# Attention with a residual on one core: the second scores of a step moved behind the values, and the last pair's final products in halves

## The chip, the cores and the metric

The kernel runs on one core of a Trainium2 chip. The core has five engines with a queue of their own each: TensorE (PE, matmuls), VectorE (DVE), ScalarE (ACT), GpSimd (POOL) and SyncE (SP, which here starts transfers). Work on one engine runs in the order in which it was put there; engines wait for each other through semaphores. The metric is the device time of one execution in microseconds (us), the median of the runs shown.

## The reference

`x` has 64 batches of 128 tokens with 512 features. For each batch the kernel adds to `x` the result of an attention layer with 16 heads of 64 features that share one key and one value, and with one extra "null" key and value (`cond`) ahead of the 128 real ones:

```python
xn = layernorm(x, g_in)
q = (xn @ Wq).reshape(b, n, H, DH).transpose(0, 2, 1, 3) * scale
kv = xn @ Wkv
k, v = (kv[..., :DH], kv[..., DH:])
...
sim = jnp.einsum('bhid,bjd->bhij', q, k)
...
sim = jnp.where(causal_mask, neg, sim)
...
attn = jax.nn.softmax(sim, axis=-1)
out = jnp.einsum('bhij,bjd->bhid', attn, v)
out = out.transpose(0, 2, 1, 3).reshape(b, n, INNER)
out = out @ Wo
return layernorm(out, g_out)
```

All of it is in float32. The output is `x` plus this.

## The kernel before, in words

The order of all work is written out by hand: nothing is rescheduled, and each engine's queue holds its instructions in the order in which the functions below are called. Semaphore waits are derived from the tiles that instructions read and write.

Batches go through in pairs. Step `d` (1 to 32) has three pairs in flight: the scores and the softmax of batches `a = 2d` and `b = 2d + 1`, the values and the output projection of the pair `p = 2d - 2`, and the normalisation, residual and store of the pair `l = 2d - 4`. Up to step 29 a step is `turn(d)` and `body(d)`, with the query products of a later pair between. Steps 30 and 31 have no query products left: they are `turn_end(d)` and `body_end(d)`, where `last` is true for step 31. Step 32 is `turn_end(32)`, which only makes the values of the last pair, and `body_last()`. The change touches these last three steps.

What a step does, by the names that follow:

- `scores(b, hf)` is the product of queries and keys for a half `hf` of the query rows: the first half (`hf` 0) needs 64 keys, the second (`hf` 1) 128. They go to PSUM rooms: those of the first halves are `ps_y` "Y" and `ps_w` "w" for a, `ps_q` "a" and `ps_w` "w" for b; the second half of a has the bank `ps_s` "s", that of b `ps_y` "X" and `ps_q` "c". `scores_add` (DVE, L667 and L669) adds mask and bias, `scores_max` (DVE, L674) takes the row maximum, `exps` (ACT, L683) the exponentials, eight rows of heads to a half, `rinv` (DVE, L701) the reciprocal of the sums, and `scale` (POOL, L705) multiplies by it.
- `blocks_T` (DVE, L721) transposes 32 by 32 blocks of the scaled weights for the product with the values; `lo` and `hi` are its two halves of rows.
- `values_rooms` gives the pair p four PSUM rooms, "a", "w", "Y", "w", each one tile for both batches. `values` (PE, L781) makes attention weights times values. `values_out_one` copies the result into the tile `oT` and adds the null value: rooms 0 and 2 by ACT (L800), rooms 1 and 3 by DVE (L798).
- The output projection of a pair is a Strassen-like scheme of seven products of 128 x 512 by 512 x 256: `out_product(p, k)` (PE, L868) is product k, four matmuls of 256 columns (two records each in the trace). `out_sum(p, k)` (L848) makes the sums of `oT` that they need: sum 0 by DVE in these steps, sums 1 to 3 by POOL; product 6 needs sum 1, product 7 sum 2, product 4 sum 3. Products 1, 6, 7 and 4 accumulate in one PSUM bank, and between them the bank is copied (`out_keep`: ACT L882, DVE L880) or added (`out_part`: DVE L898, ACT L896). Products 5 and 3 share another bank.
- `late_stats`, `late_nmr` and `late_norm` (DVE, ACT) normalise an output, `late_gain` (DVE, L1093) multiplies by `g_out`, `late_residual` (POOL, L1096) adds `x` and starts the store. `load_res` (SP) fetches that `x`.

In `turn_end(31)` as it is before, the second half of the scores of batch b stands ahead of the values, and the pending `blocks_T` of the pair p (`late_T`) stands between the row maxima. `body_end(30)` ends with the gains and residual adds of its pair l, batches 56 and 57. `body_last` ends with products 7 and 4 of the last pair, each over all 256 columns, the statistics (`bn_stats`) of each half of the output as it is ready, `late_first` and `late_second` for batch 62, and then the same two passes, and the stores, for batch 63 in halves.

Of the kernel before, what the change touches and what calls it, by code (L numbers as in the profile page):

```python
# [8 lines left out]
FP = mybir.dt.float32  # L9
U8 = mybir.dt.uint8  # L10
AF = mybir.ActivationFunctionType
ALU = mybir.AluOpType
# [5 lines left out]
def kernel(  # L18
# [698 lines left out]
    def blocks_T(b, lo=0, hi=R8):  # L717

        if lo == 0:
            sbs[b] = hp.tile([P, 6, R8, Q], FP, tag="sb", name=f"sb_{b}")  # L720
        nc.vector.transpose(  # L721
            sbs[b][:, :, lo:hi].rearrange("p j e q -> p e j q"),
            S[b][:, lo:hi, 1 : ROW - 1].rearrange("p e (j k) -> p e j k", k=Q),
        )
# [122 lines left out]
        )[k]  # L847
        eng.tensor_tensor(o, a, b, op)  # L848

    def out_product(p, k, pool, tag, start=True):  # L850
        key = "y" + tag
        if start and pool is ps_s:
            two = ps_s.tile([P, 2, DIM], FP, tag="s", name=f"py_{p}_{k}_s")
            prod[key] = two[:, 0, 0:HE]
        elif start:
            prod[key] = pool.tile([P, HE], FP, tag=tag, name=f"py{tag}_{p}_{k}")
        a, b = oT[p], oT[p + 1]
        h, w = {
            1: (a[:, 0], e11),
            2: (a[:, 1], e21),  # L860
            3: (a[:, 1], e22),
            4: (b[:, 1], sums_e[3]),
            5: (yS.get(p), sums_e[0]),
            6: (a[:, 0], sums_e[1]),
            7: (b[:, 0], sums_e[2]),
        }[k]
        for c in range(HC):
            nc.tensor.matmul(  # L868
                prod[key],
                h[:, c, :],  # L870
                w[:, c, :],
                start=(start and c == 0),
                stop=(c == HC - 1),
                skip_group_check=not start,
            )
# [8 lines left out]
    def out_part(b, e, tag, name=None):  # L884
        if b not in ys:
            if B - 6 <= b < B - 2:
                ys[b] = gp.tile(
                    [P, DIM], FP, tag=f"xS{b - B + 7}", name=f"y_{b}", bufs=1
                )
            elif b == B - 1:  # L890
                ys[b] = gp.tile([P, DIM], FP, tag="xT", name=f"y_{b}")
            else:
                ys[b] = hp.tile([P, DIM], FP, tag="y", name=f"y_{b}", bufs=3)
        o = ys[b][:, lo_e if e == 0 else hi_e]
        if name is None:
            nc.scalar.copy(o, prod["y" + tag])  # L896
        else:
            nc.vector.tensor_tensor(o, prod["y" + tag], kept.pop(name), ALU.add)  # L898
# [52 lines left out]
        )  # L951

    PAIRS = B // 2
    late_T = []

    def turn(d):

# [26 lines left out]
    def turn_end(d):  # L984

        a, b, p = 2 * d, 2 * d + 1, 2 * d - 2
        if d == PAIRS:
            blocks_T(*late_T.pop())
            late_nmr(p - 3)
            late_norm(p - 3)  # L990
            late_gain(p - 4)
            late_residual(p - 4, nc.gpsimd)
            values_rooms_apart(p)
            result_room(p)
            for m in (p, p + 1):
                values(m)
                values_out_one(m)
            return
        scores(a, 0, ((ps_y, "Y"), (ps_w, "w")))
        scores(b, 0, ((ps_q, "a"), (ps_w, "w")))  # L1000
        scores(a, 1)
        scores(b, 1, ((ps_y, "X"), (ps_q, "c")))
        scores_add(a, 0)
        scores_add(b, 0)
        scores_max(a, 0)
        if late_T:
            blocks_T(*late_T.pop())
        scores_max(b, 0)
        scores_add(a, 1)
        po = values_rooms(p)  # L1010
        values(p)
        values(p + 1)
        if d + 1 < PAIRS:
            bias_add(a + 2)
        exps(a, 0, 0, 7)
        result_room(p)
        values_out_one(p, (0, 1))
        exps(a, 0, 7)
        values_out_one(p + 1)
        values_out_one(p, (2, 3))  # L1020
        rinv(a, 0)
        out_sum(p, 0, nc.vector)
        scores_add(b, 1)

    def body_first():

# [72 lines left out]
    def body_end(d):  # L1099

        a, b, p, l = 2 * d, 2 * d + 1, 2 * d - 2, 2 * d - 4
        last = d + 1 == PAIRS
        lo, hi = (0, R8 // 2), (R8 // 2, R8)
        for r in range(p, B if last else p + 2):
            load_res(r)
        scores_max(a, 1)
        late_stats(l if last else l + 1)
        out_product(p, 1, ps_s, "s")
        exps(b, 0, 0, 4)
        out_keep("s", "yp1", "yp1")  # L1110
        exps(b, 0, 4)
        out_sum(p, 1)
        scale(a, 0)
        out_product(p, 2, ps_w, "w")
        out_part(p, 0, "w", "yp1")
        out_sum(p, 2)
        pair_pow(l if last else l + 1)
        rinv(b, 0)
        out_sum(p, 3)
        scale(b, 0)  # L1120
        scores_max(b, 1)
        out_product(p, 6, ps_s, "s", start=False)
        out_keep("s", "yu2", "yu2")
        exps(a, 1, *lo)
        rinv(a, 1, *lo)
        scale(a, 1, *lo)
        late_nmr(l)
        out_product(p, 5, ps_y, "Y")
        exps(a, 1, *hi)
        rinv(a, 1, *hi)  # L1130
        scale(a, 1, *hi)
        out_keep("Y", "yp5", "yp5")
        if last:
            late_stats(l + 1)
        else:
            late_nmr(l + 1)
        out_product(p, 7, ps_s, "s", start=False)
        exps(b, 1, *lo)
        out_part(p + 1, 1, "s", "yp5")
        rinv(b, 1, *lo)  # L1140
        scale(b, 1, *lo)
        blocks_T(a, *lo)
        blocks_T(a, *hi)
        out_product(p, 3, ps_y, "Y", start=False)
        exps(b, 1, *hi)
        rinv(b, 1, *hi)
        scale(b, 1, *hi)
        out_part(p, 1, "Y", "yu2")
        late_norm(l)
        if last:  # L1150
            pair_pow(l + 1)
        else:
            late_norm(l + 1)
        blocks_T(b, *lo)
        late_T.append((b, *hi))
        out_product(p, 4, ps_s, "s", start=False)
        out_part(p + 1, 0, "s")
        if not last:
            for m in (l, l + 1):
                late_gain(m)  # L1160
                late_residual(m, nc.gpsimd)

    def body_last():

        p = B - 2
        y = p - 2
        st = [
            small.tile([P, 2, 6], FP, tag=f"stl{i}", name=f"stl{i}", bufs=1)
            for i in range(2)
        ]  # L1170
        out_sum(p, 0, nc.vector)
        late_stats(y)
        out_product(p, 1, ps_q, "c")
        out_keep("c", "yp1", "yp1")
        out_sum(p, 1)
        pair_pow(y)
        late_stats(y + 1)
        out_product(p, 2, ps_w, "w")
        out_part(p, 0, "w", "yp1")
        nc.vector.bn_stats(st[0][:, 0], ys[p][:, lo_e])  # L1180
        out_sum(p, 3)
        pair_pow(y + 1)
        out_product(p, 5, ps_y, "Y")
        out_keep("Y", "yp5", "yp5")
        late_first(y)
        out_sum(p, 2)
        out_product(p, 6, ps_q, "c", start=False)
        late_gain(y - 1)
        late_nmr(y + 1)
        late_norm(y + 1)  # L1190
        late_second(y)
        out_keep("c", "yu2", "yu2")
        late_residual(y - 1, nc.gpsimd)
        out_product(p, 3, ps_y, "Y", start=False)
        late_gain(y + 1, nc.gpsimd)
        late_residual(y + 1, nc.gpsimd)
        out_part(p, 1, "Y", "yu2")
        nc.vector.bn_stats(st[0][:, 1], ys[p][:, hi_e])
        out_product(p, 7, ps_q, "c", start=False)
        out_part(p + 1, 1, "c", "yp5")  # L1200
        mv, rstd = last_stats(p, st[0])
        nc.vector.bn_stats(st[1][:, 1], ys[p + 1][:, hi_e])
        out_product(p, 4, ps_q, "c", start=False)
        yn[p] = mv, rstd
        late_first(p)
        late_second(p)
        x0 = prod["yc"]
        y = ys[p + 1]
        nc.vector.bn_stats(st[1][:, 0], x0)
        mv, rstd = last_stats(p + 1, st[1])  # L1210
        for half, src in ((hi_e, y[:, hi_e]), (lo_e, x0)):
            nc.vector.scalar_tensor_tensor(
                y[:, half], src, mv[:, 0:1], gob[:, half], ALU.subtract, ALU.mult
            )
        r = res.pop(p + 1)
        for half, queue in ((hi_e, nc.sync), (lo_e, nc.scalar)):
            nc.vector.scalar_tensor_tensor(
                y[:, half], y[:, half], rstd, r[:, half], ALU.mult, ALU.add
            )
            queue.dma_start(out=out[p + 1][:, half], in_=y[:, half])  # L1220
# [400 lines left out]
```

## Time and profile before

| | |
|---|---|
| median of 3 runs | 1029.53 us (1029.39 to 1029.55) |
| the profiled execution | 1029.77 us |
| its span in the trace | 1027.9 us |
| PE, PEld (weight load) busy | 1018.8 us (99%), 899.6 us (88%) |
| DVE, ACT, POOL busy | 799.0, 699.1, 745.2 us |
| `turn_end(31)` | scores from about 987.1, product 1 of the pair at 993.64 |
| `body_last` | product 1 at 1008.98, last product at 1020.19 |
| DVE's last pass | 1023.92 to 1024.80 |

Times of the trace count from the start of the span. A row of a timeline has the start, the length, the engine, the line of the kernel before, the operation, the tiles out and in, their shapes, how many instructions were merged into the row, and, in brackets, the idle time of that engine before it with what ended it. The chain of work that ended last is the path followed back from the last instruction; its rows have the start, the length on the path, engine, tile and line. `PE` is the matmul pipeline, `PEld` the weight load beside it.

### The profile page before, as it was taken

How to read it: one execution, taken by the hardware profiler on the slowest of the kernel's cores; microseconds unless marked ns; L12 is line 12 of the kernel's file. 1: busy time of each engine (PE TensorE's matmuls, PEld its weight loads, DVE VectorE, ACT ScalarE, POOL GpSimd, SP SyncE). 2: the span in 40 equal slices, each digit the busy share in tenths (PEclk: the TensorE clock that was granted, in tenths of full speed). 3: DMA queues.
4: the chain of work that ended last, by engine and by line, in shares of the span. 5: the costliest groups of instructions: out<-in, count | busy, mean ns of one | idle time of the engine just before them, and what ended most of it. 6: DMA issues, size and time to landing. Idle time of an engine off the chain costs nothing.

```text
span 1027.9 us, 31287 instructions
## 1 busy us (share of the span) xinstructions
PE 1018.8 (99%) x12345; PEld 899.6 (88%) x12345; DVE 799.0 (78%) x1774; ACT 699.1 (68%) x2805; POOL 745.2 (72%) x579
## 2 busy tenths in 40 slices
PE   9999999999999999999999999999999999999997
PEld 9888888888888888888888888888888888888886
DVE  6877777877778877788777788777888777877697
ACT  5766678666678666786666786666776667856582
POOL 4997768686686857758677686776868678586676
PEclk9999999999999999999999999999999999999999
DMA  6514152141522315233141421415223151230211
GB/s 212 144 56 127 66 152 87 53 129 64 163 77 92 99 59 167 68 108 114 45 150 67 134 99 49 140 63 158 83 76 108 60 172 69 94 90 25 82 63 63
DMA packets 73834, 100.85 MB, mean 98 GB/s; under 512 B 32212, under 2 KB 36056, under 8 KB 71896
## 3 DMA queue, kind: packets, MB, share of 16 engines
q1 hardware_dynamic: 73392, 98.47, 30.8%
q8 instruction: 96, 1.57, 0.6%
q14 instruction: 50, 0.41, 0.1%
q10 hardware_dynamic: 296, 0.40, 0.1%
HBM read 63.19 MB, written 33.55 MB: 94 GB/s over the span
## 4 chain that ended last, share of the span: by engine, by line
PE 97%; DVE 1%; POOL 1%; issue 0%; POOLq 0%; DVEq 0%
PE pa L515 20%; PE pyX L868 19%; PE pyY L868 10%; PE pc L515 10%; PE po L781 7%; PE pkv L363 6%; PE pyw L868 5%; PE pl L581 4%; PE pq L450 3%; PE ps L652 3%; PE sc_X L652 2%; PE sc_Y L652 2%; PE py_s L868 1%; PE sc_a L652 1%; PE sc_w L652 1%; PE busy L1453 1%
## 5 line engine op out<-in xcount | busy, mean ns | idle before, releaser
L683 ACT ACTIVATE s<-s,nmax 128x65 f32<-128x65 f32 (+1 forms) x1024 | 372.0, 367 | 62.4 <-DVE nmax L674 62.4
L705 POOL TENSOR_TENSOR s<-s,rinv 128x512 f32<-128x512 f32 (+1 forms) x132 | 190.8, 1448 | 151.0 <-DVE rinv L701 151.0
L617 POOL TENSOR_TENSOR s<-biasp,mneg 128x1552 f32<-128x1552 f32 (+1 forms) x65 | 205.9, 3171 | 51.2 <-DVE s L667 38.2
L683 ACT ACTIVATION_READ_ACCUMULATOR s<-s,nmax 128x1 f32 x1024 | 194.6, 190 | 0.0
L533 ACT COPY qT<-pa 128x256 f32<-128x256 f32 x59 | 22.0, 373 | 147.2 <-PE pa L515 147.2
L674 DVE TENSOR_REDUCE nmax<-s 128x8 f32<-128x1032 f32 (+1 forms) x128 | 121.4, 949 | 0.1
L515 PE MATMUL pa<-xS,wq 128*128 128x256 f32 x472 | 121.2, 379 | 0.0
L721 DVE STREAM_TRANSPOSE sb<-s 128x1536 f32<-128x1536 f32 (+1 forms) x68 | 113.5, 1672 | 2.0 <-POOL s L705 2.0
L868 PE MATMUL pyX<-wT,oT 128*128 128x256 f32 x464 | 109.7, 379 | 0.0
L868 PE MATMUL pyX<-wo,oT 128*128 128x256 f32 x464 | 109.7, 379 | 0.0
L515 PEld LDWEIGHTS pa<-xS,wq 128*128 128x128 f32 x472 | 87.2, 190 | 11.1 <-issue 0.2
L868 PEld LDWEIGHTS pyX<-wo,oT 128*128 128x128 f32 x464 | 86.0, 190 | 10.5
L868 PEld LDWEIGHTS pyX<-wT,oT 128*128 128x128 f32 x464 | 85.9, 190 | 10.6
L848 POOL TENSOR_TENSOR oT<-oT 128x512 f32<-128x512 f32 x64 | 80.6, 1277 | 3.9 <-PE pyw L868 1.6
L781 PE MATMUL po<-sb,vr 32*64 32x256 f32 (+1 forms) x4064 | 81.4, 300 | 0.0
L781 PEld LDWEIGHTS po<-sb,vr 32*64 32x64 f32 x4064 | 70.9, 130 | 8.4 <-issue 5.3
L597 DVE TENSOR_TENSOR qT<-pl,kp 128x128 f32<-128x128 f32 x112 | 31.2, 279 | 58.6 <-PE pl L581 56.0
L800 ACT ACTIVATE oT<-po,nv 128x512 f32<-128x512 f32 (+1 forms) x127 | 73.7, 654 | 0.1
L536 DVE TENSOR_TENSOR qT<-pc,ku 128x256 f32<-128x256 f32 x118 | 48.5, 411 | 32.5 <-PE pc L515 18.1
L281 POOL TENSOR_TENSOR rstd<-rstd,nhalf 128x1 f32<-128x1 f32 x64 | 35.1, 555 | 52.5 <-DVE rstd L280 43.6
L363 PE MATMUL pkv<-xT,wkv 128*128 128x256 f32 x256 | 63.3, 391 | 0.0
L527 ACT COPY ku<-pa 128x256 f32<-128x256 f32 x118 | 43.4, 368 | 28.3 <-PE pa L515 23.8
(186 smaller groups left out, 2419.2 us busy)
## 6 DMA issues: line engine op xcount, KB each, us to landing
res<-in_x_dram SPq DMA_DIRECT2D x64, 256.0 KB
x<-in_x_dram SPq DMA_DIRECT2D x63, 256.0 KB
out_dram<-y SPq DMA_DIRECT2D x63, 256.0 KB
xd<-xb SPq DMA_DIRECT2D x14, 1024.0 KB
xT<-xd SPq DMA_DIRECT2D x56, 256.0 KB
vr<-vd SPq DMA_DIRECT2D x64, 128.0 KB
kT<-kT SPq DMA_DIRECT2D x32, 64.0 KB
vd<-vb SPq DMA_DIRECT2D x32, 64.0 KB
```

Source lines behind the costliest of these rows:

```text
L363: nc.tensor.matmul(pkv, wkv[:, kc, :], xT[g][:, t : t + 2, kc, :], start=(kc == 0), stop=(kc == KC - 1),)
L515: nc.tensor.matmul(prod[tag], w[:, kc, f * P : (f + 1) * P], t[:, :, kc, :], start=(start and kc == 0), stop=(kc == HK - 1), skip_group_ch ...
L617: nc.gpsimd.tensor_tensor(S[b][:, :, keys], biasp[:, :, keys], mneg[:, t, keys] .unsqueeze(1) .broadcast_to([P, R8, keys.stop - keys.start ...
L652: nc.tensor.matmul(home[r][u * DH : (u + 1) * DH, f, :], qT[g, f, t // 2][rows, t % 2, hf, u], kT[rows, 0 : nk // Q, t, :], start=True, st ...
L674: nc.vector.tensor_reduce(nmax[b][:, hf], S[b][:, :, WITH_NULL[hf]], AX.X, ALU.max, negate=True)
L683: nc.scalar.activation(row, row, AF.Exp, bias=nmax[b][:, hf, k : k + 1], accum_out=rsum[b][:, hf, k : k + 1],)
L705: nc.gpsimd.tensor_tensor(sv, sv, rinvs[b, hf][:, lo:hi].unsqueeze(2).broadcast_to([P, hi - lo, sv.shape[2]]), ALU.mult,)
L721: nc.vector.transpose(sbs[b][:, :, lo:hi].rearrange("p j e q -> p e j q"), S[b][:, lo:hi, 1 : ROW - 1].rearrange("p e (j k) -> p e j k", k=Q),
L781: nc.tensor.matmul(po[s][rows, to : to + n], vr[g][quad, t, PLACE[j], :], sb[quad, slots, r * NF : (r + 1) * NF, :], start=(turn == 0), st ...
L800: nc.scalar.activation(to, src, AF.Identity, bias=nv2)
L848: eng.tensor_tensor(o, a, b, op)
L868: nc.tensor.matmul(prod[key], h[:, c, :], w[:, c, :], start=(start and c == 0), stop=(c == HC - 1), skip_group_check=not start,)
```

## The change

In `turn_end` (steps 30 and 31): `scores(b, 1)` goes behind the values; the transposes of b's upper rows, which step 31 did between its maxima, are done at the end of `body_end(30)`; `scores_max(b, 0)` goes behind the copies of the values; these copies (`values_out_one`) go in after the first and the fourth of the exponentials of `a`, batch by batch; DVE's `out_sum(p, 0)` goes ahead of `rinv(a, 0)`; and the gains and residual adds that `body_end(30)` did at its end are done at the end of `turn_end(31)`. In `body_last`: products 7 and 4 are each made as two halves of 128 columns, with the add, or the statistics, of a half behind it; the statistics of batch 62 are closed between the two halves of product 7.

```diff
-    def out_product(p, k, pool, tag, start=True):
+    def out_product(p, k, pool, tag, start=True, cols=slice(0, HE)):
...
             nc.tensor.matmul(
-                prod[key],
+                prod[key][:, cols],
                 h[:, c, :],
-                w[:, c, :],
+                w[:, c, cols],
...
     # out_part: the tile y of the last batch is made in body_last instead
-            elif b == B - 1:
-                ys[b] = gp.tile([P, DIM], FP, tag="xT", name=f"y_{b}")
...
     # turn_end
         scores(a, 1)
-        scores(b, 1, ((ps_y, "X"), (ps_q, "c")))
         scores_add(a, 0)
         scores_add(b, 0)
         scores_max(a, 0)
-        if late_T:
-            blocks_T(*late_T.pop())
-        scores_max(b, 0)
         scores_add(a, 1)
-        po = values_rooms(p)
+        values_rooms(p)
         values(p)
         values(p + 1)
+        scores(b, 1, ((ps_y, "X"), (ps_q, "c")))
         if d + 1 < PAIRS:
             bias_add(a + 2)
-        exps(a, 0, 0, 7)
+        exps(a, 0, 0, 1)
         result_room(p)
-        values_out_one(p, (0, 1))
-        exps(a, 0, 7)
+        values_out_one(p)
+        exps(a, 0, 1, 4)
         values_out_one(p + 1)
-        values_out_one(p, (2, 3))
+        scores_max(b, 0)
+        exps(a, 0, 4)
+        out_sum(p, 0, nc.vector)
         rinv(a, 0)
-        out_sum(p, 0, nc.vector)
         scores_add(b, 1)
+        for m in late_gains:
+            late_gain(m)
+            late_residual(m, nc.gpsimd)
+        late_gains.clear()
...
     # body_end
         blocks_T(b, *lo)
-        late_T.append((b, *hi))
+        if last:
+            late_T.append((b, *hi))
+        else:
+            blocks_T(b, *hi)
+            late_gains.extend((l, l + 1))
         out_product(p, 4, ps_s, "s", start=False)
         out_part(p + 1, 0, "s")
-        if not last:
-            for m in (l, l + 1):
-                late_gain(m)
-                late_residual(m, nc.gpsimd)
...
     # body_last
-        out_product(p, 7, ps_q, "c", start=False)
-        out_part(p + 1, 1, "c", "yp5")
-        mv, rstd = last_stats(p, st[0])
-        nc.vector.bn_stats(st[1][:, 1], ys[p + 1][:, hi_e])
-        out_product(p, 4, ps_q, "c", start=False)
-        yn[p] = mv, rstd
+        y = ys[p + 1] = gp.tile([P, DIM], FP, tag="xT", name=f"y_{p + 1}")
+        x0 = prod["yc"]
+        yp5 = kept.pop("yp5")
+        for i in range(2):
+            out_product(p, 7, ps_q, "c", start=False, cols=parts[i])
+            nc.vector.tensor_tensor(
+                y[:, parts[2 + i]], x0[:, parts[i]], yp5[:, parts[i]], ALU.add
+            )
+            if i == 0:
+                yn[p] = last_stats(p, st[0])
         late_first(p)
+        for i in range(2):
+            nc.vector.bn_stats(st[1][:, 2 + i], y[:, parts[2 + i]])
         late_second(p)
-        x0 = prod["yc"]
-        y = ys[p + 1]
-        nc.vector.bn_stats(st[1][:, 0], x0)
+        for i in range(2):
+            out_product(p, 4, ps_q, "c", start=False, cols=parts[i])
+            nc.vector.bn_stats(st[1][:, i], x0[:, parts[i]])
         mv, rstd = last_stats(p + 1, st[1])
```

The lines that name a function (`# turn_end` and the like) and `...` stand for what is left out.

More of the change, by code (lines that the diff above doesn't have):

```diff
@@ L953 @@
     PAIRS = B // 2
-    late_T = []
+    late_T, late_gains = [], []
     def turn(d):
@@ L1167, in body_last @@
         st = [
-            small.tile([P, 2, 6], FP, tag=f"stl{i}", name=f"stl{i}", bufs=1)
+            small.tile([P, 2 + 2 * i, 6], FP, tag=f"stl{i}", name=f"stl{i}", bufs=1)
             for i in range(2)
         ]
+        parts = [slice(i * P, (i + 1) * P) for i in range(4)]
         out_sum(p, 0, nc.vector)
```

## The prediction

> **What bounds the kernel now.** I read the page first: the shares of the engines, and the chain of work that ended last.
>
> ```profile
> PE 1018.8 (99%) x12345; PEld 899.6 (88%) x12345; DVE 799.0 (78%) x1774; ACT 699.1 (68%) x2805; POOL 745.2 (72%) x579
> PE 97%; DVE 1%; POOL 1%; issue 0%; POOLq 0%; DVEq 0%
> ```
>
> TensorE (PE) is busy for 99% of the span and makes 97% of the chain. So a change can only win what PE still idles, and anything that makes PE wait is paid in full. PE's timeline from step 30 on (start, length, what it is, and in brackets the idle time before it with what ended it):
>
> ```profile
> 974.79 1.97 PE L868 MATMUL py_s<-wo,oT 128*128 128x256 f32 x8 [0.61 <-DVE oT L798]
> ...
> 978.32 1.89 PE L868 MATMUL py_s<-wT,oT 128*128 128x256 f32 x8
> ...
> 993.64 1.97 PE L868 MATMUL py_s<-wo,oT 128*128 128x256 f32 x8 [0.78 <-DVE oT L798]
> 995.44 1.89 PE L868 MATMUL pyw<-wo,oT 128*128 128x256 f32 x8
> 997.17 1.89 PE L868 MATMUL py_s<-wT,oT 128*128 128x256 f32 x8
> ...
> 1008.98 1.99 PE L868 MATMUL pyc<-wo,oT 128*128 128x256 f32 x8
> ...
> 1017.71 1.89 PE L868 MATMUL pyc<-wo,oT 128*128 128x256 f32 x8
> 1020.19 1.99 PE L868 MATMUL pyc<-wT,oT 128*128 128x256 f32 x8 [0.58 <-DVE y L898]
> ```
>
> Three gaps are in reach: 0.61 and 0.78 us ahead of product 1 in steps 30 and 31, and 0.58 us ahead of product 4 in the last pair, 1.97 us in all. Whole products follow each other every 1.73 us (997.17 less 995.44).
>
> **Step 30: what the second scores behind the values do.** These rows are of the chain, VectorE (DVE) and ScalarE (ACT):
>
> ```profile
> 970.58 0.41 DVE L667 TENSOR_TENSOR s<-sc_a,s 128x256 f32<-128x256 f32 x1
> 970.85 0.10 PE sc_X L652 x2
> 971.72 2.41 PE po L781 x121
> 974.16 1.66 DVE L798 TENSOR_SCALAR oT<-po,nv 128x256 f32<-128x256 f32 x4 [0.83 <-PE po L781]
> ...
> 971.63 0.35 ACT L683 ACTIVATE s<-s,nmax 128x65 f32<-128x65 f32 x1 [2.34 <-DVE nmax L674]
> 971.97 0.34 ACT L683 ACTIVATE s<-s,nmax 128x65 f32<-128x65 f32 x1
> 974.16 0.47 ACT L800 ACTIVATE oT<-po,nv 128x256 f32<-128x256 f32 x1
> 975.93 0.36 ACT L683 ACTIVATE s<-s,nmax 128x65 f32<-128x65 f32 x1
> 977.26 0.36 ACT L882 COPY kyp<-py_s 128x256 f32<-128x256 f32 x1
> ```
>
> The values write the PSUM rooms that the first score sums read, so they can begin once the last of these adds ends, 970.58 + 0.41 = 970.99. Before, the second scores (970.85 to 971.72, 0.87 us) covered that. Now the values run from 971.05 to 973.46 and the scores to about 974.4; product 1 starts there, 0.4 us sooner than 974.79. So far the gap is filled.
>
> The price is on ACT. The row of DVE at 974.16 had idled 0.83 us for the values, and begins 0.03 us after the end of both batches' values (971.72 + 2.41 = 974.13), though it reads the first batch only. Each room is one tile for both batches, and a reader waits for its last matmul. The changed kernel puts ACT's copies of the first batch (`values_out_one(p)`) after one exponential instead of seven. ACT does one from 971.63, then stands until 973.5. Four copies and one exponential took 975.93 - 974.16 = 1.77 us; six more exponentials at 0.335 us (971.97 less 971.63, rounded) make 2.0. The first half's exponentials of batch a therefore end at 973.5 + 1.77 + 2.0 = 977.3, 1.35 us later than at 975.93.
>
> Product 6 accumulates in the bank of product 1 and waits for ACT's copy of it (977.26 before). That copy stands behind four exponentials of batch b: 977.3 + 1.35 = 978.65, and ends at 979.0. Product 6 could run at 974.4 + 2 x 1.73 = 977.85 and now runs at 979.05, 0.75 us later than 978.32. The gap closed ahead of product 1 opens again two products on, larger. I take this at its full price; it would be nothing if ACT had slack, but it has none: 975.93 and four exponentials make 977.27, where its copy began.
>
> **From step 30 to step 31.** The rows that hand over:
>
> ```profile
> 983.75 0.19 ACT L683 ACTIVATION_READ_ACCUMULATOR s<-s,nmax 128x1 f32 x1
> 984.34 1.81 DVE L721 STREAM_TRANSPOSE sb<-s 128x768 f32<-128x768 f32 x2
> 986.08 0.14 DVE L701 RECIPROCAL rinv<-rsum 128x4 f32<-128x4 f32 x1
> 986.29 1.05 POOL L705 TENSOR_TENSOR s<-s,rinv 128x512 f32<-128x512 f32 x1 [0.18 <-DVE rinv L701]
> 987.33 1.25 DVE L1093 TENSOR_TENSOR y<-y,gob 128x512 f32<-128x512 f32 x2
> 988.50 0.42 DVE L667 TENSOR_TENSOR s<-sc_w,s 128x256 f32<-128x256 f32 x1
> 990.43 0.97 DVE L721 STREAM_TRANSPOSE sb<-s 128x768 f32<-128x768 f32 x1
> ```
>
> The row of ACT ends the exponentials of batch b's lower four rows, 983.94; with ACT 1.35 late that is 985.3. DVE's reciprocal for them goes ahead of its transposes, which start at about 985.35 instead of 984.34. So the next reciprocal goes from 986.08 to 987.1, and GpSimd's (POOL) last scale runs from 987.3 to 988.35. Its transpose, which stood inside step 31 (990.43), now stands right behind it, 988.4 to 989.25. The two gains (1.17 us, 987.33 to 988.50) have left this place. So the score adds of step 31 start at 989.25 instead of 988.50: +0.75, in spite of the gains' leaving. Adds of four times 0.33 end at 990.65, values 990.7 to 993.15, second scores to 994.05: product 1 of step 31 at 994.05, +0.4 against 993.64.
>
> **Step 31: the gains and residuals in front of POOL's products.** This is the largest term.
>
> ```profile
> 988.06 2.90 POOL L1096 TENSOR_TENSOR y<-y,res 128x512 f32<-128x512 f32 x2 [0.72 <-DVE y L1093]
> 995.68 1.28 POOL L848 TENSOR_TENSOR oT<-yS,oT 128x512 f32<-128x512 f32 x1 [4.73 <-PE py_s L868]
> 1000.89 4.08 POOL L705 TENSOR_TENSOR s<-s,rinv 128x512 f32<-128x512 f32 x4
> 1005.50 1.04 POOL L705 TENSOR_TENSOR s<-s,rinv 128x512 f32<-128x512 f32 x1 [0.53 <-DVE rinv L701]
> ...
> 995.25 0.68 DVE L667 TENSOR_TENSOR s<-sc_c,s 128x512 f32<-128x512 f32 x1
> 1008.33 1.27 POOL L1096 TENSOR_TENSOR y<-y,res 128x512 f32<-128x512 f32 x1 [1.28 <-DVE y L1093]
> 1015.34 1.63 DVE L1231 SCALAR_TENSOR_TENSOR y<-y,lrs,res 128x512 f32<-128x512 f32 x1
> ```
>
> In both kernels POOL's queue has the two residual adds (2.90 us) ahead of `out_sum(60, 1)`, the row at 995.68, whose result product 6 reads. Before, they ran from 988.06 in a hole: POOL then idled 4.73 us. Now DVE's gains stand at the end of `turn_end(31)`, behind `scores_add(b, 1)`, which stands behind `rinv(a, 0)`, which needs ACT's eight exponentials. By step 30's arithmetic: values end 993.15, ACT 993.2 + 3.77 = 997.0, reciprocal to 997.1, two adds of 0.6 to 998.3, gains to 998.9 and 999.5. POOL starts the first residual at 999.0, ends the second at 999.0 + 2.90 = 1001.9, and `out_sum` at 1003.15. PE has done products 1 and 2 by 994.05 + 3.46 = 997.5 and waits about 5.6 us. Product 6 goes from 997.17 to 1003.15: +6.0.
>
> Behind it POOL is the tight engine: from 995.68 it ran without a hole to 1000.89 + 4.08 = 1004.97, and the last scale ended at 1006.54, on which the last values wait. All that moves by 1001.9 - 995.68 = 6.2, and PE's own products by 6.0. The two agree, so product 1 of the last pair goes from 1008.98 to about 1015.25: +6.3, a tenth being added for the reciprocal between two scales. Bounds: residuals at 1.27 each, as the lone one at 1008.33 shows, make it 5.9; half a microsecond more on DVE's queue makes it 6.8. SyncE's queue has the stores of these residuals ahead of the last four `load_res`; those move some 10 us, but their first reader is DVE at 1015.34, itself moved by 6, so about 2 us stay; I cost that at nothing.
>
> **The last pair: products in halves.** The order of the changed program with its waits shows that the halves are not free of each other: each half's first matmul waits for DVE, since both lie in one PSUM tile. Half 7b waits for the add of 7a, 4a for the add of 7b, 4b for the statistics of 4a.
>
> ```profile
> 952.00 0.67 PE pl L581 x6
> L597 DVE TENSOR_TENSOR qT<-pl,kp 128x128 f32<-128x128 f32 x112 | 31.2, 279 | 58.6 <-PE pl L581 56.0
> 1019.71 0.42 DVE L898 TENSOR_TENSOR y<-pyc,kyp 128x256 f32<-128x256 f32 x1 [0.91 <-PE pyc L868]
> 1020.69 0.74 DVE L1224 SCALAR_TENSOR_TENSOR y<-y,mvo,gob 128x512 f32<-128x512 f32 x1
> 1022.22 0.43 DVE L1209 BATCH_NORM_STATS2 stl<-pyc 128x6 f32<-128x256 f32 x1
> ```
>
> Matmul records of 128 columns come every 0.112 us (0.67 / 6), so a half of eight takes 0.89, plus 0.16 to its end. An add of 128 columns is 0.28, and hand-overs cost about 0.05 (1019.71 + 0.42 to 1020.19). With T the start of product 7: 7a ends T + 1.05, its add T + 1.37, 7b ends T + 2.48, its add T + 2.80, 4a ends T + 3.91. DVE meanwhile goes from T + 2.72 through the first normalising pass (0.68), two small statistics (0.2 each) and the second pass (0.68) to T + 4.5; only then comes the statistic of 4a, some 0.3 long. 4b starts at T + 4.85 and ends at T + 5.9. The last statistic starts there; before it was at 1022.22 = T + 4.51. That is 1.4 later, less 0.13 for its smaller size: +1.3. Free halves would give about -0.3.
>
> **The sum.** 6.3 + 1.3 = +7.6 us. The profiled execution took 1029.77 us around a span of 1027.9, the median of the runs is 1029.53; on the median I predict 1037.1. A measurement of this kernel can tell 0.2%, 2.06 us, from no change.
>
> **The rivals.** First, the clock. The forecast holds PE at full clock through a wait of 5.5 us without a matmul. The trace has one such wait, after the last matmul (1020.19 + 1.99 = 1022.18):
>
> ```profile
> 1026.00:1027.00 1.00, 0.00 (x0) 0.00 (x0) 0.00 (x0) 0.00 (x0) 0.00 (x0) 1.00 0.14 49
> 1027.00:1027.90 0.90, 0.00 (x0) 0.00 (x0) 0.00 (x0) 0.00 (x0) 0.00 (x0) 0.68 0.03 9
> ```
>
> The granted clock (third figure from the right) is 1.00 to 1027.0 and averages 0.68 after it: a fall to a half at about 1027.3, 5.1 us after the last matmul. The wait in step 31 is as long. If the clock falls in it, products restart at half speed; 3 to 6 us of that cost 1 to 3 us, as PE and POOL are level there: 1038.1 to 1040.1, about 1038.9. Chance 0.37. [...]
>
> Second, the other side: POOL is not held, because the gains end before product 1 does. Then the three gaps close, 1029.5 - 2.0 = 1027.5. It decides at the end of the second residual: at 995.7 or sooner nothing is lost. By the rows it comes 6 us too late. For it speaks that residuals had a hole of 4.73 us before. Chance 0.04.
>
> Third, the copies wait only for their own batch: ACT stays on time, the residuals end some 2 us sooner, and the sum is about 5.5: 1035.0. The 0.83 us that DVE idled speaks against it. Chance 0.06. Fourth, halves that don't wait: 1035.5, chance 0.03.
>
> **Numbers.** The forecast keeps 0.50. The range 1035.4 to 1040.2 holds it with its bounds (5.9 to 6.8 on the large term, about a microsecond either way on the rest), nearly all of the clock's case and the fourth; the second and third rival and the edges, some 0.2, stay outside. Faster by over 0.2%: 0.02, half of the second rival; within 0.2%: 0.03; slower: 0.95.
>
> **What would show it.** In PE's waits a new one of 5 to 6 us, product 6 of step 31 behind POOL's `oT`; the residuals of POOL at about 999 instead of 988; ACT idle 1.5 us ahead of its first copy in steps 30 and 31; and waits of PE between the halves, the last about 1 us, behind the statistics. A granted clock under 1 around 1003 shows the first rival. The forecast is wrong if the residuals run before 996, or if the halves follow each other without idle time.

## The result and the profile after

| | before | after |
|---|---|---|
| median | 1029.55 us (1029.39 to 1029.73, 5 runs) | 1038.96 us (1038.63 to 1040.02, 5 runs) |
| ratio, 95% interval | | 1.0092 [1.0080, 1.0103] |
| profiled execution, its span | 1029.77, 1027.9 us | 1039.19, 1037.1 us |

The change costs 9.4 us. The forecast was 1037.1 with a range of 1035.4 to 1040.2; what came is the forecast's mechanism together with the first rival, which stood at about 1038.9. The page of the changed kernel, the busy times and the shares of the chain of work that ended last:

```profile
PE 1021.3 (98%) x12361; PEld 901.5 (87%) x12361; DVE 799.9 (77%) x1777; ACT 698.9 (67%) x2805; POOL 745.0 (72%) x579
PE 94%; issue 2%; POOL 2%; DVE 1%; ACT 0%; DMA 0%; POOLq 0%; DVEq 0%
```

DVE, ACT and POOL do the same work as before. TensorE (PE) is 2.5 us longer busy and its share of the chain falls from 97% to 94%. So the time went into PE's waits, and a smaller part into PE being slower. PE's waits by what ended them (total, times, longest):

```profile
PE py_s L868 <- POOL oT L848: 5.5, 1, 5.5
...
PE py_s L868 <- ACT kyp L882: 0.9, 1, 0.9
PE pyc L868 <- DVE y L1205: 0.8, 2, 0.5
PE pyc L868 <- DVE stl L1216: 0.8, 1, 0.8
PE po L781 <- PE ps L652: 0.5, 1, 0.5
PE po L781 <- DVE s L667: 0.3, 1, 0.3
```

Each of the waits that the prediction named is here: product 6 of step 31 behind POOL's sum, product 6 of step 30 behind ACT's copy, the three between the halves. The gaps of 0.61 and 0.78 us ahead of product 1 are gone. Their places on PE's timeline, products 1 and 6 of step 30, 1 and 6 of step 31, 1 of the last pair, and the four halves:

```profile
974.44 1.99 PE L868 MATMUL py_s<-wo,oT 128*128 128x256 f32 x8
...
979.07 1.97 PE L868 MATMUL py_s<-wT,oT 128*128 128x256 f32 x8 [0.90 <-ACT kyp L882]
...
994.32 1.99 PE L868 MATMUL py_s<-wo,oT 128*128 128x256 f32 x8
...
1003.51 3.52 PE L868 MATMUL py_s<-wT,oT 128*128 128x256 f32 x8 [5.47 <-POOL oT L848]
...
1016.81 1.99 PE L868 MATMUL pyc<-wo,oT 128*128 128x256 f32 x8
...
1025.55 1.05 PE L868 MATMUL pyc<-wo,oT 128*128 128x128 f32 x8
1027.05 1.16 PE L868 MATMUL pyc<-wo,oT 128*128 128x128 f32 x8 [0.45 <-DVE y L1205]
1028.59 1.16 PE L868 MATMUL pyc<-wT,oT 128*128 128x128 f32 x8 [0.38 <-DVE y L1205]
1030.51 1.16 PE L868 MATMUL pyc<-wT,oT 128*128 128x128 f32 x8 [0.76 <-DVE stl L1216]
```

Two things are to be seen. Product 6 of step 31 starts at 1003.51, where the forecast said 1003.15. And it takes 3.52 us instead of 1.97. The windows of one microsecond around it, with the granted clock as the third figure from the right, say why:

```profile
1002.00:1003.00 1.00, 0.00 (x0) 0.00 (x0) 1.00 (x4) 1.00 (x6) 1.00 (x2) 1.00 0.57 219
1003.00:1004.00 1.00, 0.49 (x1) 0.49 (x2) 0.58 (x1) 1.00 (x7) 1.00 (x2) 0.61 0.73 279
1004.00:1005.00 1.00, 1.00 (x4) 0.73 (x4) 0.00 (x0) 0.26 (x2) 1.00 (x2) 0.50 1.00 348
1005.00:1006.00 1.00, 1.00 (x4) 0.82 (x3) 0.00 (x0) 0.00 (x0) 1.00 (x2) 0.50 0.88 252
1006.00:1007.00 1.00, 1.00 (x5) 0.80 (x4) 0.00 (x0) 0.00 (x0) 1.00 (x2) 0.68 0.90 248
1007.00:1008.00 1.00, 1.00 (x7) 0.87 (x6) 0.93 (x5) 0.00 (x0) 1.00 (x2) 1.00 0.46 176
```

The windows at 1004 and 1005 show 0.50, half speed, so an average of 0.61 is full speed for 0.22 us and half for 0.78. So the clock fell at 1003.22, 5.2 us after the last matmul had ended (1003.51 - 5.47 = 998.04), and 0.3 us before product 6 could start. Half speed lasted 0.78 + 1 + 1 + 0.64 = 3.42 us.

The rows of POOL, DVE and ACT that lead there:

```profile
999.37 2.87 POOL L1096 TENSOR_TENSOR y<-y,res 128x512 f32<-128x512 f32 x2 [10.98 <-DVE y L1093]
1002.20 1.26 POOL L848 TENSOR_TENSOR oT<-yS,oT 128x512 f32<-128x512 f32 x1
...
1013.34 1.04 POOL L705 TENSOR_TENSOR s<-s,rinv 128x512 f32<-128x512 f32 x1 [0.74 <-DVE rinv L701]
```

```profile
989.32 0.39 DVE L667 TENSOR_TENSOR s<-sc_w,s 128x256 f32<-128x256 f32 x1
...
997.33 0.20 DVE L701 RECIPROCAL rinv<-rsum 128x8 f32<-128x8 f32 x1 [0.64 <-ACT s L683]
...
998.61 1.28 DVE L1093 TENSOR_TENSOR y<-y,gob 128x512 f32<-128x512 f32 x2
...
1031.71 0.30 DVE L1216 BATCH_NORM_STATS2 stl<-pyc 128x6 f32<-128x128 f32 x1 [1.25 <-PE pyc L868]
```

```profile
973.46 0.84 ACT L800 ACTIVATE oT<-po,nv 128x256 f32<-128x256 f32 x2 [1.55 <-PE po L781]
...
978.56 0.36 ACT L882 COPY kyp<-py_s 128x256 f32<-128x256 f32 x1
```

POOL idles 10.98 us for DVE's gains, and only then does the two residual adds and the sum that PE waits for. ACT idles 1.55 us for the values, and its copy for product 6 comes 1.3 us later than before (977.26).

### The profile page after: what moved, and what is told of

Its sections match the earlier page's. It is cut to its first block, busy times and chain, and to the rows that moved or that the text cites. A ratio compares the mean times of both kernels' runs of the same rounds, so it can differ in the third digit from the quotient of the medians.

```text
span 1037.1 us, 31319 instructions
## 1 busy us (share of the span) xinstructions
PE 1021.3 (98%) x12361; PEld 901.5 (87%) x12361; DVE 799.9 (77%) x1777; ACT 698.9 (67%) x2805; POOL 745.0 (72%) x579
## 4 chain that ended last, share of the span: by engine, by line
PE 94%; issue 2%; POOL 2%; DVE 1%; ACT 0%; DMA 0%; POOLq 0%; DVEq 0%
PE pa L515 20%; PE pyX L868 19%; PE pc L515 10%; PE pyY L868 10%; PE po L781 7%; PE pkv L363 6%; PE pyw L868 5%; PE pl L581 4%; PE pq L450 3%; PE ps L652 3%; PE sc_X L652 2%; PE sc_Y L652 2%; PE sc_a L652 1%; PE py_s L868 1%; PE sc_w L652 1%
```

## The experiments

Theory: the late gains put the residual adds in front of POOL's sum; the early copies delay ACT; the halves wait for each other in their one PSUM tile; and the clock falls in the long wait. Each is tried by itself. Beside the runs below, the kernel before took 1029.77 to 1029.82 us in the median, a quarter of a microsecond more than in the table above, so a difference to the changed kernel is known to some 0.3 us. The ratios are to the kernel before as run beside each.

**The gains back at the end of `body_end(30)`,** the rest as changed:

```diff
         scores_add(b, 1)
-        for m in late_gains:
-            late_gain(m)
-            late_residual(m, nc.gpsimd)
-        late_gains.clear()
...  # body_end
             blocks_T(b, *hi)
-            late_gains.extend((l, l + 1))
...
         out_part(p + 1, 0, "s")
+        if not last:
+            for m in (l, l + 1):
+                late_gain(m)
+                late_residual(m, nc.gpsimd)
```

> The changed kernel (1038.96 us) with one part undone: the gains and residual adds of batches 56 and 57 stand at the end of step 30 again. Theory 1 (residuals ahead of POOL's sum, and the clock's fall that the wait causes, make most of the loss; ACT's late copies and the halves make the rest): PE's wait of 5.5 us in step 31 is gone, no wait is over 2 us, the granted clock stays 1.00 until the end; but the gains now delay step 31's score adds again, and ACT's copies and the halves stay, so about 1034.1 us. Theory 2 (the late copies cost nothing, since PE has product work to do meanwhile): only the halves stay, about 1031 us. Theory 3 (the residuals are not what POOL waits behind): no change, about 1039 us.

Measured: 1034.53 us, 1.0046 [1.0031, 1.0061], 4.4 less than the changed kernel and near the 1034.1 of the first theory. PE's waits and DVE's gains in this kernel:

```profile
PE py_s L868 <- ACT kyp L882: 1.8, 2, 0.9
PE po L781 <- issue: 1.7, 1, 1.7
```

```profile
989.39 1.25 DVE L1089 TENSOR_TENSOR y<-y,gob 128x512 f32<-128x512 f32 x2
990.56 0.42 DVE L667 TENSOR_TENSOR s<-sc_w,s 128x256 f32<-128x256 f32 x1
```

The wait for POOL is gone. A new one of 1.7 us stands ahead of the values of step 31, which the profile puts down to "issue"; the values start 0.1 us after the last score add, and these adds begin at 990.56, behind the gains, where the changed kernel had them at 989.32. ACT's copy now delays product 6 in both steps.

**The residual adds left out.** The adds of batches 56 and 57 are not done (their output lacks `x`); the gains stay late.

```diff
             late_gain(m)
-            late_residual(m, nc.gpsimd)
+            res.pop(m)
+            store(m)
```

> The changed kernel, with the residual adds of batches 56 and 57 left out (their gains and stores stay where the change put them). Theory 1 (POOL's sum waits behind the residual adds): PE's wait of 5.5 us goes, waits of 1.2 to 1.4 us behind ACT's and DVE's copies of the accumulating bank take its place, the clock does not fall: about 1034.0 us. Rival (the gains on DVE, not the residuals on POOL, hold step 31): 1038 us or more.

Measured: 1037.18 us, 1.0071 [1.0056, 1.0086]. Neither text was right: only 1.8 us of the changed kernel's time went. PE, DVE and POOL of this kernel:

```profile
1005.50 2.59 PE L868 MATMUL py_s<-wo,oT 128*128 128x256 f32 x8 [2.81 <-DVE rinv L701]
```

```profile
998.58 2.74 DVE L1094 TENSOR_TENSOR y<-y,gob 128x512 f32<-128x512 f32 x2
1001.25 1.22 DVE L674 TENSOR_REDUCE nmax<-s 128x8 f32<-128x1032 f32 x1
```

```profile
998.05 1.05 POOL L705 TENSOR_TENSOR s<-s,rinv 128x512 f32<-128x512 f32 x1
999.05 1.72 POOL L848 TENSOR_TENSOR oT<-oT 128x512 f32<-128x512 f32 x1
```

POOL's sum is no longer late, but POOL now works while DVE does its gains, and both take longer: two gains take 2.74 us (1.07 and 1.75) instead of 1.28, and a sum 1.72 instead of 1.26. The rows fit a wait of DVE for POOL: the two gains need about 0.6 us each, and if the first waited for the rest of a scale (998.58 to 999.10) and the second for that of a sum (some 1.1 us, to 1000.77), that makes 2.8. This is the author's reading of the rows; no run tests it. The row maxima behind them come 1.44 us later (1001.25 against 999.81 in the changed kernel), and PE waits 2.81 us two products on, ahead of product 7, for which DVE copies the bank behind its next maxima. So by this reading about 1.4 of the 2.81 us come from this collision. And the clock fell again:

```profile
1006.00:1007.00 1.00, 1.00 (x5) 0.86 (x4) 0.82 (x3) 1.00 (x6) 1.00 (x2) 0.85 0.47 180
...
1010.00:1011.00 1.00, 1.00 (x6) 0.87 (x5) 0.93 (x3) 0.00 (x0) 0.26 (x2) 0.95 0.00 0
```

The windows between show 0.50. Half speed for 0.3 + 3 + 0.1 = 3.4 us, after a wait of only 2.81 us and when PE had been back at work for 1.2 us. Products 7 and 3, which ran in it, took 1.7 us longer together (2.59 and 2.99 us instead of 1.97 and 1.89). So the gains have a price of their own at that place, which the residual adds hide in the changed kernel.

**PE kept busy through the wait,** by 22 matmuls whose result nobody reads:

```diff
         out_product(p, 2, ps_w, "w")
+        if last:
+            fill = ps_w.tile([P, P], FP, tag="w", name="fill")
+            for _ in range(22):
+                nc.tensor.matmul(fill, ident, ident, start=True, stop=True)
```

> The changed kernel with 22 extra matmuls of 128 columns on PE behind product 2 of step 31 (their result is not used), about 5 us of work in a wait of 5.5 us. Theory 1 (the wait without matmuls lets the clock fall, and that costs 1.5 us): product 6 of step 31 starts at the same time, takes 1.97 us instead of 3.52, the granted clock stays 1.00 to the end, and the time is about 1037.4 us, with a spread of the runs as small as that of the kernel before. Rival (POOL sets the pace behind the wait, so the clock costs nothing): 1038.8 to 1039.0 us.

Measured: 1037.46 us, 1.0075 [1.0062, 1.0089], 1.5 less than the changed kernel, though PE does more. Product 6 starts where it did and has its old length, and the granted clock is 1.00 from 998 to 1012:

```profile
1003.39 1.99 PE L868 MATMUL py_s<-wT,oT 128*128 128x256 f32 x8 [0.48 <-POOL oT L848]
```

So the clock's price is about 1.5 us, and without it the change takes almost what the forecast said. That agrees with product 6 of the changed kernel, which was 1.55 us longer.

**The copies behind seven exponentials,** on top of the gains back:

```diff
-        exps(a, 0, 0, 1)
+        exps(a, 0, 0, 7)
         result_room(p)
         values_out_one(p)
-        exps(a, 0, 1, 4)
+        exps(a, 0, 7)
         values_out_one(p + 1)
         scores_max(b, 0)
-        exps(a, 0, 4)
```

> As e1_gains_back, and in addition ACT's and DVE's copies of the values stand behind seven exponentials of a as before, and the reciprocal's place is kept. Theory 1 (the early copies make ACT stand for 1.5 us in each of steps 30 and 31): about 1032.0 us, 2 us under e1_gains_back. Rival (the copies' place costs nothing): the same time as e1_gains_back.

Measured: 1032.71 us, 1.0029 [1.0018, 1.0040]: 1.8 less than with the gains back alone. Both waits for ACT's copy (1.8 us together) are gone and nothing of their size took their place (two of 0.2 us behind POOL's sum are new). So the early copies cost some 0.9 us in each of the two steps where nothing else hides them; the 1032.0 us expected were 0.7 too low.

**The halves alone,** on the kernel before: the part of the change in `body_last` and nothing else.

> The kernel before (1029.55 us) with the halves of products 7 and 4 alone. Theory 1 (the halves wait for each other): 1030.9 to 1031.2 us. Theory 2 (the halves close the gap of 0.58 us): 1029.0 to 1029.3 us.

Measured: 1031.48 us, 1.0016 [1.0007, 1.0026], +1.7 us: the first theory, and a little above its range. The waits between the halves are the same 0.5, 0.4 and 0.8 as in the changed kernel.

**The whole products back** in the changed kernel: `body_last` as before.

> The changed kernel with products 7 and 4 of the last pair whole again and the order of the last pair's statistics as before. Theory 1 (halves wait for each other through DVE and cost 1.3 to 1.6 us): about 1037.5 us, and one wait of PE of about 0.6 us ahead of product 4 in place of three. Theory 2 (halves cost nothing, or gain 0.3): 1039.0 to 1039.3 us.

Measured: 1038.48 us (1037.60 to 1038.72), 1.0083 [1.0067, 1.0098]: 0.5 less than the changed kernel, not the 1.5 expected. The profiled execution shows why:

```profile
1003.38 3.78 PE L868 MATMUL py_s<-wT,oT 128*128 128x256 f32 x8 [5.37 <-POOL oT L848]
1006.95 2.85 PE L868 MATMUL pyY<-wT,yS 128*128 128x256 f32 x8
```

```profile
1002.00:1003.00 1.00, 0.00 (x0) 0.00 (x0) 1.00 (x3) 1.00 (x7) 1.00 (x2) 0.53 0.45 174
...
1008.00:1009.00 1.00, 1.00 (x5) 0.80 (x4) 0.81 (x3) 0.00 (x0) 1.00 (x2) 0.56 0.00 0
```

The same wait cost two slow products here, because the clock was half from 1002.06 to 1008.88 (all windows between show 0.50), 6.8 us, twice as long. Products 6 and 5 were 1.81 and 0.96 us longer, against 1.55 in the changed kernel. What the tail won, the clock took for the most part in this execution; for the other three the windows aren't known. The tail by itself is better read from the run before this one.

**The halves in two PSUM tiles,** on the kernel before: products 1, 6, 7 and 4 of the last pair accumulate their two halves in different tiles.

```diff
+        halves = (ps_q, "c"), (ps_y, "X")
...
+                prod[key] = pool.tile([P, P], FP, tag=tag, name=f"py{tag}_{p}_{k}")
...
         for i in range(2):
-            out_product(p, 7, ps_q, "c", start=False, cols=parts[i])
+            acc(7, i)
```

> The kernel before with the halves of products 7 and 4 and, for the last pair, the accumulating products 1, 6, 7 and 4 in two PSUM tiles of 128 columns each. Theory 1 (the halves wait for each other only because they share a tile): no wait of PE in the last pair is over 0.1 us, and as DVE is then the bound there, about 1029.3 us. Rival (halves cost by themselves, in matmuls or in DVE's smaller operations): over 1030 us.

Measured: 1030.09 us, 1.0002 [0.9994, 1.0011]: no gain and no loss that can be told, where the first theory expected 1029.3. PE's last half, and DVE's passes over batch 62 and last statistics:

```profile
1020.49 1.06 PE L870 MATMUL pyX<-wT,oT 128*128 128x128 f32 x8
```

```profile
1020.01 1.25 DVE L1246 SCALAR_TENSOR_TENSOR y<-y,mvo,gob 128x512 f32<-128x512 f32 x1
...
1021.70 0.75 DVE L1253 SCALAR_TENSOR_TENSOR y<-y,rstdo,res 128x512 f32<-128x512 f32 x1
1022.37 0.29 DVE L1231 BATCH_NORM_STATS2 stl<-pyc 128x6 f32<-128x128 f32 x1
1022.58 0.28 DVE L1231 BATCH_NORM_STATS2 stl<-pyX 128x6 f32<-128x128 f32 x1
```

The halves now follow each other without a wait, so the waits did come from the shared tile (or from its bank: the two tiles lie in two pools, and the run doesn't tell these apart). But PE ends at 1021.55 and the last statistics start at 1022.37, behind DVE's pass over batch 62: DVE sets the end here, and before it was nearly the same (1022.22). Half a microsecond of this is in the pass at 1020.01, which took 1.25 us instead of the 0.74 that it has before. Before, it starts at 1020.69, when POOL's residual add has just ended (1019.41 + 1.27 = 1020.68); here it starts 0.68 us sooner. That it met the add, as the gains met POOL's work in the run without the residual adds, is the author's estimate.

**The second scores behind the values, alone,** on the kernel before:

```diff
         scores(a, 1)
-        scores(b, 1, ((ps_y, "X"), (ps_q, "c")))
...
         values(p + 1)
+        scores(b, 1, ((ps_y, "X"), (ps_q, "c")))
```

> The kernel before with one line moved: the second scores of batch b behind the values, in steps 30 and 31. Theory 1 (this alone fills the gaps ahead of product 1, and is harmless): the waits of 0.61 and 0.78 us go, PE waits instead about 0.3 us (step 30) and 1.0 us (step 31) for the first score adds ahead of the values: 1029.3 us, 0.2 to 0.3 under the kernel before. Rival (the move itself harms by holding the values): 1029.8 us or more.

Measured: 1029.53 us beside 1029.77 for the kernel before, 0.9997 [0.9989, 1.0006]: the same within what can be told. The two gaps ahead of product 1 are gone, and PE waits 0.3 and 0.9 us ahead of the values instead. The gaps were moved and, at 1.2 us instead of 1.39, hardly made smaller. The 0.24 us between the medians is what the first theory expected, but the interval doesn't tell it from nothing.

**The last two together, with batch 62's first pass sooner:**

> The kernel before, with the second scores of batch b behind the values in steps 30 and 31, the last pair's products 1, 6, 7 and 4 in two halves of 128 columns that lie in two PSUM tiles, and the statistics of batch 62 closed, and its first pass done, ahead of the adds of batch 63's upper half. Theory: the scores' move wins about 0.3 us on PE that the end of the kernel gave back, and the halves apart take PE's last wait; with DVE's passes of batch 62 sooner, the last statistic is no longer late: 1028.8 to 1029.2 us. Rival: DVE sets the end whatever PE does, and nothing of it can be measured: 1029.5 to 1029.8.

Measured: 1029.99 us, 0.9999 [0.9990, 1.0008]: as the rival said, nothing can be measured, and the 1028.8 to 1029.2 us of the theory didn't come. DVE and POOL of this kernel:

```profile
1019.28 1.79 DVE L1247 SCALAR_TENSOR_TENSOR y<-y,mvo,gob 128x512 f32<-128x512 f32 x1
```

```profile
1019.26 1.26 POOL L1096 TENSOR_TENSOR y<-y,res 128x512 f32<-128x512 f32 x1
```

The pass that was put sooner met POOL's residual add and took 1.79 us instead of the 0.74 that it has before: it ended at 1021.07, 0.55 us after the add (1020.52). The add for the second half stood behind it, and PE waited 0.75 us for that add: the wait between the halves was back, by another way. So whether the halves apart can win the 0.3 us is not settled by these two runs.

**The change with its gains ahead of the values:** whole products, copies behind seven exponentials, reciprocal and sum in the order of before, and

```diff
         scores_add(a, 1)
+        for m in late_gains:
+            late_gain(m)
+            late_residual(m, nc.gpsimd)
+        late_gains.clear()
         values_rooms(p)
```

> The changed kernel with three things otherwise: products 7 and 4 of the last pair whole, as before; the copies of the values behind seven exponentials, as before; and the gains and residual adds of batches 56 and 57 ahead of the values of step 31, right behind the four score adds, where DVE waits for PE anyway. Theory: the place of the gains (behind the exponentials) is what made the large term, and ahead of the score adds they still cost some 1.2 us of DVE's time on the path; behind the adds they are free. Residual adds from about 991 to 994, ahead of POOL's sum: 1029.1 to 1029.6 us, no wait of PE over 1 us. Rival: what was left over, some 1.2 us, is the cost of the transposes in front of the score adds, and stays: 1030.8 to 1031.2.

Measured: 1029.98 us (1029.65 to 1030.85), 1.0000 [0.9991, 1.0009]. Between the two expectations: the rival's 1030.8 to 1031.2 us didn't come, and of the 1029.1 to 1029.6 expected the win of 0.2 to 0.7 us isn't seen. POOL's residual adds, then products 7 of step 31 and 1 of the last pair:

```profile
991.90 2.89 POOL L1098 TENSOR_TENSOR y<-y,res 128x512 f32<-128x512 f32 x2 [4.72 <-DVE y L1095]
```

```profile
1000.71 1.97 PE L868 MATMUL py_s<-wo,oT 128*128 128x256 f32 x8 [0.17 <-DVE rinv L701]
...
1008.98 1.99 PE L868 MATMUL pyc<-wo,oT 128*128 128x256 f32 x8
```

The residual adds run in a hole of POOL's and end at 994.8, ahead of the sum. All 9 us of the change are gone, and nothing is won: product 1 of the last pair stands at 1008.98 as before. Product 1 of step 31 was 0.5 us sooner (993.12 against 993.64), but product 7 waits for DVE and starts at 1000.71 against 1000.70. DVE has no hole in either kernel from the score adds to the copy that product 7 needs (1000.15 against 1000.14): it did the same work in another order, so the gains were not free there but took the place of the transposes. That the two times agree to a hundredth is chance; in the two runs that change only the tail, the same product stands at 1009.29 and 1008.86.

## Why the prediction was right, and where it was short

The steps, predicted and measured in the trace, in the prediction's order:

| step | predicted | measured |
|---|---|---|
| product 1, step 30 | 974.4 | 974.44 |
| product 6, step 30 | 979.05 | 979.07 |
| score adds of step 31 start | 989.25 | 989.32 |
| product 1, step 31 | 994.05 | 994.32 |
| residual adds | 999.0 to 1001.9 | 999.37 to 1002.24 |
| PE's wait | 5.6 | 5.47 |
| product 6, step 31 | 1003.15 | 1003.51 |
| product 1 of the last pair | +6.3 | +7.83 |
| last statistic after the start of product 7 | 5.9 | 6.16 |

- **The large term** was sized right up to product 6, within 0.4 us. What failed is the sum's "+6.3" behind it, which held PE at full clock: the trace has +7.83 (1016.81 against 1008.98), and product 6 alone was 1.55 longer. The run with PE kept busy puts the clock's part at 1.5 us. This was the first rival with its price of 1 to 3 us; it had a chance of 0.37 where the forecast kept 0.50. No run that was known then shows the 3 to 6 us at half speed behind that price; the later ones showed 3.4 to 6.82 us, at 1.55 to 2.77 us. So the point of 1037.1 was the wrong one of the two, and the range held because it was made to take in the rival. The one distance that the prediction had, 5.1 us from the last matmul to the fall against a wait of 5.5, made the case look closer than it was: the fall came 5.2 us after the last matmul in the changed kernel, but 4.1 with whole products and 4.0 without the residual adds. That the median came within 0.1 us of the rival's 1038.9 is partly luck: the clock cost 1.5 us instead of 1.8, and the large term and the halves made up the rest.
- **The halves** were put at 1.4 later for the last statistic and measure 1.65 (6.16 against 4.51); less the statistic's smaller size that is +1.5 where the sum had +1.3, and alone they cost 1.7. The difference is in the matmuls: each of the three halves behind a wait takes 1.16 us, not the 1.05 that the prediction used for all four. That halves without waits would win 0.3 us wasn't borne out by the run, 1.0002 [0.9994, 1.0011], and isn't excluded by it.
- **The copies** cost about what was said: 0.75 for step 30 was foreseen, and the runs give 1.8 for both steps where nothing else hides them. In the changed kernel step 31's share lies inside the wait for POOL.
- **The cause of the large term** was put on the residual adds. That they stand in front of the sum is shown by the trace. But it isn't enough to remove them: without them 1037.18 remain, since the gains meet POOL's work and delay the row maxima. The prediction named the gains' place as the cause and counted only what stood behind them on POOL; on DVE's side it had no term, because POOL was later.
- **The fetches of `x`** on SyncE's queue were put at nothing, and that held: their first reader on DVE went from 1015.34 to 1023.17, by 7.83 us, just as PE did.
- **The other rivals** fell. POOL was held, over 6 us too late (1002.24 against 995.7); ACT did wait for both batches' values; the halves did wait.

In sum, of 9.4 us, 1.5 are the clock, 1.7 the halves, and the remaining 6.2 the gains and the copies together, which agrees with the last run, where both were moved back or elsewhere and the halves undone. That the parts add up so is worked out from separate runs.

## What to carry to other kernels

An instruction that is moved behind a late result takes along all that stands behind it on the next engine's queue: here two gains of 0.6 us, put behind eight exponentials, held two adds and with them a sum that PE needed. Where the engine that bounds the kernel will stand still for some microseconds, count its slower restart as well (here 1.5 us after a wait of 5.5), and ask of each wait that goes which one comes next: the scores' move and the halves apart took gaps away from PE, and neither made the kernel faster by anything that the runs can tell. DVE's gains are best put where POOL idles: two took 1.28 us in the last run, where POOL had idled 4.72 us until the first of them was done, and 2.74 beside POOL's scale and sum in the run without the residual adds.

## What the runs showed of the hardware

- **Half speed lasted 3.4 or 6.8 us.** The granted clock was 0.50 for 3.42 us in the changed kernel, 3.4 without the residual adds and 6.82 with whole products.
- **The fall came at no fixed distance from the last matmul.** In the long waits it was 5.2 us in the changed kernel (998.04 to 1003.22), 4.1 with whole products (998.01 to 1002.06) and 4.0 without the residual adds (1002.69 to 1006.70, where PE had been back since 1005.50). At the end of the kernel it was 5.1 us before (1022.18 to 1027.3), 2.3 in the changed kernel (1031.67 to 1033.94) and 2.7 with the gains ahead of the values (1022.18 to 1024.92). With the gains back, a wait of 1.7 us brought no fall: the granted clock was 1.00 from 990 to 1027. What decides when it falls is not shown; no run varied the idle time by small steps.
- **The same wait cost 1.55 us or 2.77 us of product time.** With whole products (a wait of 5.37 us) the clock fell 1.3 us before product 6 started (1002.06 to 1003.38), and half speed lasted 6.82 us; in the changed kernel (5.47 us) it fell 0.3 us before, and half speed lasted 3.42. That such a wait makes the times scatter more isn't shown: five runs of the changed kernel lie between 1038.63 and 1040.02, but 21 later runs of the kernel before between 1029.47 and 1030.74.
- **Without the residual adds, a gain of DVE beside POOL's work took 1.4 us in the mean instead of 0.64,** and POOL's sum 1.72 instead of 1.26; a pass of 0.74 took 1.25 in the run with the halves in two tiles, and 1.79 beside POOL's residual add in the run of the last two together.
